# A graph layer on one core: seven parts instead of six, and every unit in eight steps

## The chip, the cores and the metric

The kernel runs on one core of a Trainium2 chip. The engines that matter are TensorE (PE; its weight loads are shown as PEld), VectorE (DVE), ScalarE (ACT), GpSimd (POOL) and SyncE (SP), whose queue issues nearly all the plain transfers; GpSimd issues the indirect ones. The metric is the device time of one execution in microseconds, the median of the runs shown. The profile is of one execution, with a span from the first to the last instruction that is a little shorter than that execution's own time.

## The reference

The layer has 12500 nodes with 128 features and 412500 edges with 64 features. Edges are sorted by their destination `dst`; the attention of an edge depends on both its ends and its own features, the softmax runs over all the edges at once, and the weighted values are summed by source node. Two normalisations follow.

```python
h = x @ Wn + bn
q, k, v = x @ Wq + bq, x @ Wk + bk, x @ Wv + bv
eh = edge_attr @ We + be
attn_in = concatenate([q[src], k[dst], eh], axis=-1)
hmid = leaky_relu(attn_in @ A1 + b1, 0.2)
scores = leaky_relu(hmid @ A2 + b2, 0.2)          # 8 heads
w = softmax(scores.mean(axis=-1), axis=0)         # over all edges
out = segment_sum(w[:, None] * v[dst], src)
y = h + out
ref = gamma * (y - mean(y)) / sqrt(var(y) + 1e-5) + beta
result = layernorm(x + ref)
```

## The kernel before

A1 is multiplied into Wq, Wk and We beforehand, so that an edge's hidden layer is a sum of three terms: one of its source node, one of its destination node, one of its own features. The host pads the edges to 403 groups of 1024 (8 tiles of 128), and the nodes to 98 blocks of 128: node i belongs to block i mod 98.

The work has two halves that run beside each other.

*Making records* (`make`, L749 to 962), group by group in the order of `dst`. Since `dst` is sorted, a group's destinations lie in a short window of rows. A one-hot matrix (L799) and TensorE products (L854, L860 in `rows`) give, for each edge, its destination's k-term plus its edge term, and its v row. ScalarE copies these from PSUM to a record of 260 numbers (L871; L872 adds the source's place within its block). In the meantime VectorE counts, for every block, how many edges came before (L785 to L836): this gives each edge the row of its block's region to which its record goes. GpSimd then scatters the records, 128 rows of 1040 bytes at a time, to a table in DRAM, `rtab` (L883, eight scatters for a group). The pool of records has 6 buffers of four tiles.

*Units* (`sums_of`, L980 to 1311). Once all groups of a part are in the table, a unit takes two blocks' regions of it: a load `rt` (L1016), the sources' row `sl` (L1038), which TensorE turns (L1046), VectorE writes as bytes `slT` (L1053) and SyncE puts to DRAM (`put`, L1060) and reads back to all 128 partitions as `rowB` (`spread`, L1065). From this come one-hots in chunks of four tiles (L1074), hidden layers (L1085, L1094), leaky relu (L1105, L1109), scores (L1122 to L1155), a running maximum (L1165 to L1189), weights (L1194), the weighting of source one-hots (L1203, L1217), and the weighted sums of v (L1246), which are added to the sums of the part before (L1227 loads them, L1262 adds, L1269 stores).

The groups are cut into 6 parts of 73, 73, 73, 73, 62 and 49 groups (`CUTS`, L34). A block's region in a part has as many tiles as its mean number of edges plus 4.4 standard deviations need: 7, 7, 7, 7, 6 and 5. So units have 14, 12 or 10 tiles, and there are 6 x 49 = 294 of them. Two tables are used in turn (`TABS`), with 7 tiles a block. Rows that no record may reach are filled with zeros beforehand (`fill`, L513, and `fill_piece`, L526), all of it during the first part: 54 transfers of two blocks with 2 tiles each and 44 with 3. The first part also makes the tables of node terms (`tables`, L1495) and the places of the later edges (`later`), spread over nine tenths of its groups.

There is no scheduler: the order on each engine is the order of the program. Units are planned in *steps* (L983 to L1006): a unit's operations get numbers of steps from `s0`, the step of its first hidden layer. `e` is 1 for units of four chunks and 0 for those of three; it sets how many steps lie between one engine's work and the next one's that needs it. A unit of four chunks follows the one before after 8 steps, one of three after 6. `turn` is how many steps ahead of `s0` the row is turned: 11, or 8 where `e` is 0. A load may not come before a buffer of `rt` is free (`BLKS`, 6). The loop from L1566 runs through a part's groups, in six pieces each, and spreads the steps of the units of the part before evenly between them; the first part has no units beside it, and after the sixth part its units follow alone (the tail). `closing` (L1314) then scales, adds, normalises twice and writes out, seven blocks at a time, in buffers of `rt`.

Of the kernel before, what the change touches and what calls it, by code (L numbers as in the profile page):

```python
# [10 lines left out]
FP = mybir.dt.float32  # L11
# [9 lines left out]
P = 128  # L21
# [5 lines left out]
NB = 7  # L27
GT = 8
CG = 4
BLKS = 6  # L30
XA = 3
SPAN = 42
NP = 6
CUTS = 0, 0.1811, 0.3623, 0.5434, 0.7246, 0.8784, 1  # L34
TABS = 2
WIDTH = 14
HOLD = 7
LATE = 3
R = 4
WR = 260  # L40
# [3 lines left out]
class Plan:  # L44
# [4 lines left out]
    def __init__(self, n, e, nb, groups):  # L49
        self.n, self.e, self.nb, self.groups = n, e, nb, groups  # L50
        cut = [round(groups * c) for c in CUTS]
        self.parts = list(zip(cut[:-1], cut[1:]))


        def means(g0, g1):
            return [
                (min(e, g1 * GT * P) - g0 * GT * P) * max(0, -(-(n - b) // nb)) / n
                for b in range(nb)
            ]

        self.tiles = [
            max(-(-int(np.ceil(m + 4.4 * m**0.5)) // P) for m in means(*part))
            for part in self.parts
        ]
        most = max(self.tiles)
        self.cap = most * P
        self.trash = GT * P
        self.rows = nb * self.cap + self.trash


        self.fill = [
            [min(most, -(-int(most * P - m + 4.5 * m**0.5) // P)) for m in means(*part)]
            for part in self.parts[:TABS]
        ]
# [378 lines left out]
def sorted_path(  # L453
# [8 lines left out]
    nc = tc.nc  # L462
    nb = plan.nb
# [38 lines left out]
        nc.vector.memset(headsum[32 * j : 32 * j + 32, j : j + 1], 1.0)  # L502


    fmax = max(max(f) for f in plan.fill)
    empty = None

    def empties(pool):
        nonlocal empty
        empty = pool.tile([P, fmax, WR], FP, name="empty")  # L510
        nc.vector.memset(empty, 0.0)

    def fill(k, n):  # L513

        cap = plan.cap
        b = 0
        while b < nb:
            m = 1
            while m < n and b + m < nb and plan.fill[k][b + m] == plan.fill[k][b]:
                m += 1  # L520
            f = plan.fill[k][b]
            if f:
                yield b, m, f
            b += m

    def fill_piece(k, b, m, f):  # L526
        cap = plan.cap
        piece = nc.sync.dma_start(
            out=rtab[k][b * cap : (b + m) * cap, :]
            .rearrange("(b c) w -> b c w", b=m)[:, cap - f * P : cap, :]  # L530
            .rearrange("b (p k) w -> p b (k w)", p=P),
            in_=empty[:, :f, :]
            .rearrange("p (o k) w -> p o (k w)", o=1)
            .to_broadcast([P, m, f * WR]),
        ).ins
        if k == 0:
# [443 lines left out]
    def sums_of(bp):  # L980


        plans, s0, first, free, done, starts = [], 19, None, [], [], {}  # L983
        for p, bs, t in units:
            nt = len(bs) * t
            nk = -(-nt // 4)
            L, e = 2 * nk, int(nk > 3)
            turn = 11 if e else 8
            if plans:
                s0 += 2 * plans[-1][1]  # L990


            load_at = free[-BLKS] + 1 if len(free) >= BLKS else 0
            lead = turn + 8 if p in starts or p == 0 else turn + 8 + LATE
            s0 = max(s0, load_at + lead - 1)
            if first is not None:
                s0 = max(s0, first - (L + 5 + 3 * e))
            if len(done) > 1:
                s0 = max(s0, done[-2] + 1 - (L + 4 + 2 * e))
            f = s0 + L + 5 + 3 * e  # L1000
            load_at = max(load_at, s0 - lead)
            free.append(f + 3 + e + L)
            done.append(f + 4 + e + L)
            first = f + L
            starts.setdefault(p, load_at)
            plans.append((nt, nk, s0, load_at, f, e, turn))  # L1006
        steps = {}

# [264 lines left out]
        for i, (nt, nk, s0, load_at, f, e, turn_at) in enumerate(plans):  # L1273
# [33 lines left out]
        closing(bp, do, tail, f + 3 + e, f + 5 + e + 2 * j + 4)  # L1307
        order = lambda at: [(fn, args) for _, fn, args in sorted(at, key=lambda x: x[0])]
        return [order(steps.get(s, [])) for s in range(max(steps) + 1)], [
            starts[p] for p in range(NP)  # L1310
        ]


    def closing(bp, do, s0, s1, s2):  # L1314
# [6 lines left out]
        def three(b, k):  # L1321
            return b[:, k * NB * D : (k + 1) * NB * D].rearrange("p (b d) -> p b d", d=D)
# [78 lines left out]
        def fetch(st):  # L1401
            bl = st["bl"]
            rt = bp.tile([P, TM, WR], FP, name="rt").rearrange("p t w -> p (t w)")
            for k, (name, of) in enumerate((("hs", htab), ("part", atab[NP - 1]), ("xs", xtab))):
                st[name] = three(rt, k)
                nc.sync.dma_start(out=st[name], in_=of[:, bl, :])
            st["n1"], st["o"] = three(rt, 3), st["part"]

        def spread(st, y, k):
            if k == 1:  # L1410
# [155 lines left out]
    with tc.manual_schedule():  # L1566
        done = 0
        for p in range(NP + 1):
# [118 lines left out]
```

## Time and profile before

| | us |
|---|---|
| median of three runs (lowest, highest) | 5124.87 (5107.2, 5132.39) |
| profiled execution, own time | 5108.98 |
| its span | 5107.2 |
| PE, DVE, ACT, POOL busy | 4197.8, 3989.1, 3275.2, 3347.9 |
| first scatter; last scatter | 64.7; 4480.3 |
| masks made at a part's end (L920), first and last | 837.4; 4478.4 |
| last load of a unit; end | 4927.0; 5107.2 |

An engine's busy time is a share of the whole span, and stages have different limits, so the busy time by stretch says more than the page's first line. A group's line gives its count, its busy time, the mean of one in ns, and after the second bar the time that the engine was idle just before it, with what ended most of that time; "issue" there means that the profile shows nothing that it waited for. Matmuls overlap, so TensorE's busy share is not its share of work. A row of a stretch gives its ends, its length, each engine's busy time with the number of instructions, the granted clock, the share of the DMA engines and their rate in GB/s.

### The profile page before, as it was taken

Reading aid. Unit: us, or ns where it says so; the run is one execution under the profiler, and the core shown is the slowest. Engines: PE = TensorE matmul, PEld = TensorE weight load, DVE = VectorE, ACT = ScalarE, POOL = GpSimd, SP = SyncE. Lnnn points to the kernel's source line nnn. Section 1 sums busy time; section 2 is a strip of 40 time slices with the busy share of each in tenths; the row PEclk is TensorE's granted clock in tenths of the full one; section 3 lists DMA queues with packets and bytes.
Section 4 is the critical chain, followed back from the end, with each engine's and each line's share of the span. In section 5 each row is a group of like instructions: output and inputs, shape, how many; then the busy total and the mean of one; then the engine's idle time right before and its main releaser. Section 6 shows DMA issues by size and latency. Waiting matters only on the chain.

```text
span 5107.2 us, 97900 instructions
## 1 busy us (share of the span) xinstructions
PE 4197.8 (82%) x32676; PEld 3121.7 (61%) x32676; DVE 3989.1 (78%) x10011; ACT 3275.2 (64%) x8487; POOL 3347.9 (66%) x3265
## 2 busy tenths in 40 slices
PE   4556564998998989998999998999999899988880
PEld 2333332666766767776766776677777676666660
DVE  7666663888887888888888887888888788766678
ACT  2333331666766777776777776777777677766776
POOL 3777777777777777777777777777767566611002
PEclk7666665999999999999999999999999999999995
DMA  5889895988888998998988998998998898878763
GB/s 188 281 277 314 292 336 175 323 297 296 298 302 278 316 316 308 316 304 297 322 310 306 314 314 286 315 318 311 318 316 301 291 307 305 293 248 265 247 232 139
DMA packets 589700, 1477.77 MB, mean 289 GB/s; under 512 B 102746, under 2 KB 315629, under 8 KB 587392
## 3 DMA queue, kind: packets, MB, share of 16 engines
q1 hardware_dynamic: 434224, 1042.03, 62.4%
q0 software_dynamic: 154752, 429.39, 22.0%
q8 instruction: 259, 4.24, 0.3%
q14 instruction: 257, 2.11, 0.1%
q10 hardware_dynamic: 208, 0.00, 0.0%
HBM read 890.36 MB, written 580.68 MB: 288 GB/s over the span
## 4 chain that ended last, share of the span: by engine, by line
DMA 35%; PE 19%; POOL 16%; DVE 14%; issue 9%; ACT 7%; SPq 1%; ACTq 0%; DVEq 0%; POOLq 0%
DMA rtab<-rec,idx 18%; POOL rtab L883 16%; DMA row<-slT 6%; DMA rt<-rtab 5%; PE psm L1246 4%; DMA rowB<-row 4%; PE ph L1094 3%; PE pkv L860 3%; ACT rec L871 2%; PE ph L1085 2%; ACT ohw L1217 2%; PE pkv L854 2%; DVE hm L1109 2%; PE psm L1155 2%; PE psc L1122 1%
## 5 line engine op out<-in xcount | busy, mean ns | idle before, releaser
L883 POOL DMA_INDIRECT rtab<-rec,idx x3224 | 3287.0, 1020 | 1190.9 <-issue 789.4
L871 ACT ACTIVATE rec<-pkv 128x1024 f32<-128x1024 f32 x806 | 821.6, 1019 | 1125.1 <-DMA rtab<-rec,idx 789.5
L1217 ACT ACTIVATE ohw<-ohs,w 128x128 f32<-128x128 bf16 x3822 | 1259.5, 400 | 13.2 <-PE psm L1246 1.4
L1246 PE MATMUL psm<-rt,ohw 128*128 128x128 f32 x7644 | 1150.3, 293 | 8.9 <-ACT ohw L1217 7.5
L1246 PEld LDWEIGHTS psm<-rt,ohw 128*128 128x128 f32 x7644 | 983.5, 198 | 104.2 <-ACT hm L1105 31.3
L1105 ACT ACTIVATE hm<-ph 128x512 f32<-128x512 f32 (+1 forms) x1078 | 583.4, 541 | 473.3 <-PE ph L1094 466.8
L854 PE MATMUL pkv<-kvs,ohd 128*128 128x256 bf16 x3224 | 550.0, 299 | 402.9 <-ACT rec L871 378.9
L1094 PE MATMUL ph<-ohT,qs 128*128 128x512 bf16 (+3 forms) x4116 | 819.6, 321 | 39.6 <-DVE ohT L1074 39.4
L1109 DVE TENSOR_TENSOR hm<-ph,hm 128x512 f32<-128x512 f32 (+1 forms) x1078 | 668.0, 620 | 114.9 <-ACT hm L1105 114.5
L860 PE MATMUL pkv<-WeS,eat 64*128 64x128 f32 x6448 | 658.7, 329 | 0.0
L854 PEld LDWEIGHTS <-ohd 128*128 128x128 bf16 x3224 | 321.8, 105 | 542.2 <-issue 453.1
L1085 PE MATMUL ph<-ident,rt 128*128 128x128 f32 x3822 | 622.5, 281 | 14.3 <-DVE hm L1109 13.5
L1074 DVE TENSOR_SCALAR ohT<-rowB,iotaP 128x512 bf16<-128x512 uint8 (+1 forms) x1078 | 521.8, 484 | 119.3 <-DMA rowB<-row 114.3
L860 PEld LDWEIGHTS pkv<-WeS,eat 64*128 64x128 f32 x6448 | 487.9, 213 | 201.1 <-issue 199.0
L1094 PEld LDWEIGHTS <-qs 128*128 128x128 bf16 x4116 | 395.3, 100 | 173.4 <-issue 50.8
L1085 PEld LDWEIGHTS ph<-ident,rt 128*128 128x128 f32 x3822 | 477.2, 152 | 22.5 <-DVE hm L1109 17.9
L823 DVE TENSOR_TENSOR ats<-pc,oh 128x792 f32<-128x792 f32 x403 | 392.3, 973 | 106.1 <-PE pc L805 103.5
L1203 DVE TENSOR_TENSOR ohs<-iotaE,sl 128x512 bf16<-128x512 bf16 (+1 forms) x1078 | 415.0, 385 | 51.2 <-ACT ohw L1217 50.3
L1155 PE MATMUL psm<-headsum,z 128*128 128x4 f32 (+1 forms) x2156 | 286.4, 254 | 146.0 <-DVE z L1145 65.7
L834 DVE TENSOR_REDUCE pos<-ats 128x8 f32<-128x792 f32 x403 | 389.9, 967 | 3.4
L1155 PEld LDWEIGHTS psm<-headsum,z 128*128 128x128 f32 (+1 forms) x2156 | 273.9, 198 | 176.9 <-DVE z L1145 79.1
L1122 PE MATMUL psc<-hm,A2s 128*32 128x512 f32 (+3 forms) x2352 | 319.5, 533 | 12.8 <-DVE slT L1053 7.0
(151 smaller groups left out, 4080.8 us busy)
## 6 DMA issues: line engine op xcount, KB each, us to landing
rt<-rtab SPq DMA_DIRECT2D x196, 1820.0 KB
eat<-in_ea SPq DMA_DIRECT2D x201, 512.0 KB
rt<-rtab SPq DMA_DIRECT2D x49, 1560.0 KB
rt<-rtab SPq DMA_DIRECT2D x49, 1300.0 KB
qs<-qtab SPq DMA_DIRECT2D x294, 192.0 KB
rtab<-rec,idx POOLq DMA_INDIRECT x3224
dstb<-dtab SPq DMA_DIRECT2D x201, 256.0 KB
rowB<-row SPq DMA_DIRECT2D x196, 224.0 KB
```

The source lines that it names most:

```text
L854: nc.tensor.matmul(pk[:, h, i, :], ohd[:, t * P : (t + 1) * P], kvs, start=(i == 0), stop=False,)
L860: nc.tensor.matmul(pk[:, h, i, :D], eat[h * DE : (h + 1) * DE, (j + i) * P : (j + i + 1) * P], WeS[h * DE : (h + 1) * DE, :], start=False, ...
L871: nc.scalar.activation(rec[:, :, :, : 2 * D], pk, AF.Copy)
L883: one_tile = nc.gpsimd.indirect_dma_start(out=rtab[p % TABS][:, :], out_offset=bass.IndirectOffsetOnAxis(ap=idxs[g][:, t : t + 1], axis=0) ...
L1074: nc.vector.tensor_scalar(st["oh"][k][:, : n * P], st["rowB"][:, t0 * P : (t0 + n) * P], iotaP, None, op0=ALU.is_equal,)
L1085: nc.tensor.matmul(ph[:, j * P : (j + 1) * P], st["rt"][:, t0 + j, :D], ident, is_transpose=True, start=(j == 0), stop=False,)
L1094: nc.tensor.matmul(ph[:, cols], st["qs"][:, j0 // t, s, :], oh[:, cols], start=False, stop=(s == 2 and j1 == t0 + n),)
L1105: nc.scalar.activation(hm, state[i]["ph", k][:, : n * P], AF.Copy, scale=SLOPE)
L1109: nc.vector.tensor_tensor(hm, ph[:, : n * P], hm, op=ALU.max)
L1155: nc.tensor.matmul(st["psS"][:, t0 + j : t0 + j + (nv - 1) * sw + 1 : sw], z[: 32 * nv, j * P : (j + 1) * P], headsum[: 32 * nv, :nv], sta ...
L1217: nc.scalar.activation(ohw[:, j, :], ohs[:, :, j], AF.Copy, scale=st["w"][:, t0 + j : t0 + j + 1])
L1246: nc.tensor.matmul(st["psS"][:, (1 + u) * P : (2 + u) * P], ohw[:, j, :], st["rt"][:, t0 + j, D : 2 * D], start=(k == 0), stop=(k == t - 1),)
```

## The change

The number of parts, their cuts, the margin and the number of buffers are new: 7 parts of 40, 51, 62, 62, 62, 63 and 63 groups, with a margin of 4.15 standard deviations and regions of 4, 5, 6, 6, 6, 6 and 6 tiles. Units have 8, 10 or 12 tiles, that is two or three chunks, and there are 7 x 49 = 343 of them; the sum of tiles over all units stays 3822. `rt` has 7 buffers of 12 tiles instead of 6 of 14. `e` is 1 for all units, a unit follows the one before after 8 steps whatever its size (with 4 more for each chunk that it has more), and `turn` is 14, 12 or 11 for two, three or four chunks.

Since the first two parts' regions are smaller than the largest, the filling is in two stages. During the first part the rows between the least that a block can receive and its part's own tiles are filled from a tile of zeros in SBUF, as before (98 transfers of two blocks, 2 tiles each). The tiles above that, which the table's next part uses, are filled later: during the second part for the first table (49 transfers of two blocks, 2 tiles each) and during the third part for the second one (49, 1 tile each), in the eighth to the five eighths of the part's pieces. Their source is a table of zeros in DRAM. The steps that must be done by a part's end are at least those up to the last load of the part before. In `closing`, `n1` and `o` use the tiles of `part` and `hs`, as `rt` is smaller now.

```diff
-BLKS = 6
+BLKS = 7
-NP = 6
-CUTS = 0, 0.1811, 0.3623, 0.5434, 0.7246, 0.8784, 1
+NP = 7
+CUTS = 0, 0.0993, 0.2258, 0.3797, 0.5335, 0.6873, 0.8437, 1
...
-            max(-(-int(np.ceil(m + 4.4 * m**0.5)) // P) for m in means(*part))
+            max(-(-int(np.ceil(m + 4.15 * m**0.5)) // P) for m in means(*part))
...
-    fmax = max(max(f) for f in plan.fill)
+    fmax = max(
+        max(plan.tiles[k] - plan.cap // P + max(plan.fill[k]), plan.cap // P - plan.tiles[k])
+        for k in range(TABS)
+    )
+    zeros = dram.tile([P, fmax, WR], FP, name="zeros")
...
         nc.vector.memset(empty, 0.0)
+        nc.sync.dma_start(out=zeros, in_=empty)
...
-            f = plan.fill[k][b]
-            if f:
-                yield b, m, f
+            a = plan.cap // P - plan.fill[k][b]
+            if a < top:
+                yield b, m, a, top - a
...
+    def fill_top(k, n):
+
+        top, most = plan.tiles[k], plan.cap // P
+        if top < most:
+            for b in range(0, nb, n):
+                yield b, min(n, nb - b), top, most - top
...
-            .rearrange("(b c) w -> b c w", b=m)[:, cap - f * P : cap, :]
+            .rearrange("(b c) w -> b c w", b=m)[:, a * P : (a + f) * P, :]
             .rearrange("b (p k) w -> p b (k w)", p=P),
-            in_=empty[:, :f, :]
+            in_=(empty if source is None else source)[:, :f, :]
...
-            L, e = 2 * nk, int(nk > 3)
-            turn = 11 if e else 8
+            L, e = 2 * nk, 1
+            turn = {2: 14, 3: 12, 4: 11}[nk]
             if plans:
-                s0 += 2 * plans[-1][1]
+                s0 += 8 + 4 * (nk - plans[-1][1])
...
+            ends[p] = load_at
...
-            starts[p] for p in range(NP)
+            max(starts[p] - HOLD, ends[p - 1] + 1) if p else 0 for p in range(NP)
...
-            st["n1"], st["o"] = three(rt, 3), st["part"]
+            st["n1"], st["o"] = st["part"], st["hs"]
...
-            until = 0 if p == 0 else starts[p] - HOLD if p < NP else len(steps)
+            until = 0 if p == 0 else starts[p] if p < NP else len(steps)
...
+            if 0 < p <= TABS:
+                pieces = list(fill_top(p - 1, 2))
+                fills = [
+                    (na // 8 + na * j // (2 * len(pieces)), (p - 1, *piece, zeros))
+                    for j, piece in enumerate(pieces)
+                ]
```

More of the change, by code (lines that the diff above doesn't have):

```diff
@@ L511, in empties @@
         nc.vector.memset(empty, 0.0)
+        nc.sync.dma_start(out=zeros, in_=empty)
     def fill(k, n):
-        cap = plan.cap
-        b = 0
+        b, top = 0, plan.tiles[k]
         while b < nb:
@@ L520, in fill, with fill_piece @@
                 m += 1
-            f = plan.fill[k][b]
-            if f:
-                yield b, m, f
+            a = plan.cap // P - plan.fill[k][b]
+            if a < top:
+                yield b, m, a, top - a
             b += m
-    def fill_piece(k, b, m, f):
+    def fill_top(k, n):
[3 more added lines that the diff above has]
+                yield b, min(n, nb - b), top, most - top
+    def fill_piece(k, b, m, a, f, source=None):
         cap = plan.cap
@@ L535, in fill_piece @@
         ).ins
-        if k == 0:
+        if k == 0 and source is None:
             tc.declare_no_dep(piece, group="rows0", reason="rows that no record has reached")
@@ L980, in sums_of @@
     def sums_of(bp):
-        plans, s0, first, free, done, starts = [], 19, None, [], [], {}
+        plans, s0, first, free, done, starts, ends = [], 19, None, [], [], {}, {}
         for p, bs, t in units:
```

## The prediction, made before the changed kernel ran

> **What bounds the kernel now.** I read the page first (engines by slice, costliest groups), then busy time by stretch, then what GpSimd waited for, then SyncE's queue and VectorE in order of time where GpSimd is not the limit.
>
> ```profile
> span 5107.2 us, 97900 instructions
> ...
> POOL 3777777777777777777777777777767566611002
> ...
> L883 POOL DMA_INDIRECT rtab<-rec,idx x3224 | 3287.0, 1020 | 1190.9 <-issue 789.4
> ```
>
> GpSimd sends 3224 scatters (8 for each of 403 groups). Its slices stand at 7 up to the 28th and fall only afterwards. 7 is full here, as the waits show (stretch 1610 to 3146, then 3866 to 4478):
>
> ```profile
> POOL rtab L883 <- issue: 287.2, 942, 0.3
> ...
> POOL rtab L883 <- issue: 88.9, 291, 0.5
> POOL rtab L883 <- ACT rec L872: 79.6, 47, 6.7
> ```
>
> In the first stretch nearly all its idle time is a 0.3 us gap ahead of each scatter; with 0.96 us of work that is 1.265 us, and 1.31 on average: 10.51 us for a group's eight. In the second stretch it waits for records too. Last scatters of the six parts start at 869, 1639, 2405, 3173, 3873 and 4480 us: 73 groups take 766 to 770, but 62 take 700 (10.51 x 62 would be 652) and 49 take 607 (515). So GpSimd's rate sets the first four parts, units of 14 and 12 tiles set the fifth and sixth, and 627 us follow with no scatter. The stretches:
>
> ```profile
> 66.00:440.00 374.00, 217.05 (x1174) 142.59 (x1175) 262.52 (x469) 141.53 (x178) 287.82 (x260) 0.68 0.84 281
> 440.00:760.00 320.00, 194.25 (x1010) 125.26 (x1010) 200.02 (x399) 99.74 (x157) 247.11 (x239) 0.66 0.94 322
> 760.00:837.00 77.00, 36.44 (x212) 24.06 (x211) 31.99 (x61) 19.63 (x34) 59.02 (x60) 0.51 0.49 165
> ...
> 2378.00:3146.00 768.00, 701.76 (x5773) 529.34 (x5773) 650.56 (x1598) 554.62 (x1470) 589.96 (x585) 0.96 0.90 309
> 3146.00:3866.00 720.00, 675.92 (x5496) 510.23 (x5495) 610.79 (x1528) 538.38 (x1442) 515.62 (x512) 0.96 0.90 310
> 3866.00:4478.00 612.00, 561.53 (x4578) 420.78 (x4577) 481.83 (x1233) 433.23 (x1180) 400.07 (x396) 0.97 0.88 300
> 4478.00:4927.00 449.00, 388.60 (x2952) 300.75 (x2949) 301.05 (x939) 316.64 (x947) 31.81 (x17) 0.96 0.76 250
> ```
>
> The last columns are clock, DMA share and GB/s. What paces the sixth part and the tail is a loop through two small transfers:
>
> ```profile
> 4107.65 0.34 SPq L1060 DMA_DIRECT2D row<-slT  x1
> ...
> 4113.98 0.32 SPq L1065 DMA_DIRECT2D rowB<-row  x1
> ...
> 4118.35 0.48 DVE L1074 TENSOR_SCALAR ohT<-rowB,iotaP 128x512 bf16<-128x512 uint8 x1 [0.88 <-DMA rowB<-row]
> 4118.75 0.27 DVE L1053 TENSOR_SCALAR slT<-psc 12x128 uint8<-12x128 f32 x1
> ...
> 4119.05 0.32 SPq L1060 DMA_DIRECT2D row<-slT  x1
> ```
>
> A unit's row goes out, must land before it is read back to 128 partitions, the first one-hot waits for that, and only then does VectorE make the next unit's row. Over the sixth part 6.4 + 5.3 + 0.7 = 12.4 us, its whole unit period (12.5); in the tail 4.0 + 4.0 + 0.7 = 8.7 of 9.0.
>
> **The change, part by part.** All sums go by the profiled execution, span 5107.2 us (its own time is 5109.0; the median of the runs shown, 5124.9, lies 0.3% above).
>
> *First part, 73 to 40 groups.* It has no units beside it. 33 fewer groups are 264 scatters. GpSimd alone: the part's 583 intervals take 804 us, 67 above 1.265 each. That surplus sits on the table-making (two scatters that meet a subtraction of the tables take over 2.1 us), which stays, so 320 x 1.265 + 60 = 465. Bytes: before, 73 x 1.52 (records, features, indices, rows) + 64 of fills + 49 of tables = 224 MB (the rows give 221). After: 61 + 52 (98 fills of 520 KB) + 49 = 162, all but 6 in 36 groups. At the 322 GB/s of the row 440:760, 484 us, and 42 for the last four groups: 526. At 350, about what the fullest 20 us stretches hold (344 to 376), 488. VectorE has 495 - 33 x 4.06 (a group's seven operations: 0.97, 0.97, 0.76, 0.55, 0.37, 0.27, 0.17) = 361 us of work: hidden. Take 500, from 465 to 550; its last scatter starts at 565 instead of 869.
>
> *Second part, 51 groups beside 49 units of 8 tiles.* Scatters 51 x 10.51 = 536. Bytes 78 + 49 x 1.52 = 152 MB. New: 49 copies of 520 KB from a table of zeros in DRAM, in half of this part. No row shows DRAM to DRAM. Counted once, that half moves 102 MB in 268 us, 382 GB/s: at 340, +33 us; at 375, +5; counted as read and write, 128 MB, +109. I take +40, nearest to the count that the page's bytes use: 576. Each copy also stands in SyncE's queue ahead of the next rows and loads: 0.5 us of issue (the fills' median), 49 of them 25 us in a queue that mostly waits; behind a copy still in flight, the row's read-back has waited for a transfer only 14 us in 1610:3146 (L1065 for rt). Nothing added for it; were that cover gone, rival 2's price.
>
> *Third part, 62 groups, units of 10.* 652; 26 MB/2 of copies bring its half to 332 GB/s: +8 (0 to +30): 660.
>
> *Parts four to seven: 62, 62, 63, 63 groups beside units of 12.* 652 and 662 by scatters, period 13.3 us a unit. Per group there are 9.4 tiles, as in the parts of 73, so engines and DMA (205 MB, 314 GB/s against 309) are as full as at 2378:3146. 98 fewer chunks of one-hots (980 for 1078) pay for 49 more units. The seventh buffer takes away the wait of a load for a free buffer (SyncE's L1016 waits 180 us for sums in 1610:3146). The loop of 12.4 fits under 13.3 with 0.9 to spare. +5 each (0 to +40): 657, 657, 667, 667. The margin of 4.15 moves only the caps; the rule that a part ends after the last load of the one before it moves nothing here (step 387 against 384).
>
> Last scatter: 565 + 576 + 660 + 2 x 657 + 2 x 667 = 4449, against 4480. The four wide parts recover what was lost beside the 62 and 49 groups; the copies and denser fills eat most of the shorter start.
>
> *Tail.* 49 units of 12 tiles instead of 10. TensorE is busy 388.6 of 449 us, 7.8 a unit: with 12 tiles 9.4. The loop gives some 8.9 (rowB grows from 160 to 192 KB). The two-step spacing should take away TensorE's waits for the scores (47 us here), but not the loop, since the next unit's row is made in the same step as the first one-hot, behind it, before and after. So 9.4 (9.05 to 10.86, all scaled), 48 x 0.35 = +17: 644 after the last scatter. The closing's shared buffers (n1 over part, o over hs) write over tiles whose last reader stands ahead of them in the order of steps: nothing.
>
> Sum: 4449 + 644 = 5093, 14 less than before. Own time 5095; raised by the 0.3% that the median before lies above its profile, 5110.
>
> **The rivals** (times on the median's footing).
> 1. *The gain is kept.* DMA never sets the pace: 465, 541, 652, 653, 653, 663, 663, tail 635: 65 + 4290 + 635 = 4990, as a median 5005. For it: 322 GB/s held for 320 us while groups took 10.6 us. Against: at GpSimd's pace the new first part needs 350 and half the second 382.
> 2. *The row loop sets parts four to seven.* It decides from 13.3 us a unit, 0.9 above the sixth part's. At 14.0, 49 x 14.0 = 686 a part: +29 twice, +19 twice, some 10 in the third, 106 in all: 5215, slower. For it: in the fifth part (310 GB/s) the loop was 6.3 + 6.0 + 1.4 = 13.7, and rt came late there and in the sixth (35 times, 55 us). Against: 0.7 of that was a step between one-hot and next row that units of 12 do not have, and row and rt are larger in units of 14.
> 3. *Transfers set the first parts.* First part 526, second +109, third +30: 117 more than forecast, 5225. It decides where these stages get under 320 GB/s. The Trainium skill, "DMA: Bandwidth & Descriptors" (Specifications), gives an HBM limit of about 358 GB/s per core, which a copy within DRAM would load on both sides; by it, as an estimate, that half of the second part takes 128 MB / 358 = 357 us, +89 where I take +40. The trace does not bear it out as a hard limit (376 GB/s in 380 to 400 us), and no run here has such a copy.
> 4. *The tail stays as loose as before*, 10.4 us a unit: +48, 5160.
>
> A block overflowing its smaller cap would start the second path; the inputs' fullest blocks (484 of 512, 599 of 640, 725 of 768) exclude it.
>
> **How the numbers follow.** Forecast (5070 to 5150) 0.40; kept 0.25; loop 0.17; transfers 0.12; tail 0.06. What a measurement can tell from no change is about 0.5%, 26 us: below 5099 the forecast has 0.16 of its 0.40, within 0.20, above 0.04. Faster 0.16 + 0.25 = 0.41; slower 0.04 + 0.17 + 0.12 + half of the tail's = 0.36; within 0.23. For eight in ten, 4990 (all but the end of rival 1) to 5225 (most of 2 and 3).
>
> **What would show it.** First part's last scatter near 565; second part 576, with DMA share near 1 in its first half; parts four to seven with GpSimd's gaps "issue" alone at 10.6 us a group; row to row 13.4 us there; a tail period of 9.4. Records waited for by GpSimd in parts four to seven would be rival 2; a last scatter later than 4480, or a unit period over 10 in the tail, makes the forecast wrong.

## The result, and the profile after

The changed kernel takes 5179.3 us (median of 4 runs, 5169.6 to 5186.4), the kernel before in the same session 5128.6. The ratio is 1.0117, with a 95% interval of 1.0099 to 1.0136: slower by 1.2%. The forecast was 5110, no change within what can be told. The time lies inside the range given for eight in ten (4990 to 5225), but outside the forecast's own 5070 to 5150, and both signs that were named for a wrong forecast are there: the last scatter starts after 4480, at 4509, and a unit of the tail takes 10.04 us.

From the page of the changed kernel, the span, GpSimd's busy tenths by slice and the DMA totals (before 1477.77 MB), and from its list of groups the scatters':

```profile
span 5184.7 us, 98509 instructions
...
POOL 2666766677777777777777777777777777611002
...
L894 POOL DMA_INDIRECT rtab<-rec,idx x3224 | 3298.0, 1023 | 1209.2 <-issue 757.4 <-ACT rec L883 146.1 <-DMA rtab<-empty 61.5
...
DMA packets 658349, 1528.11 MB, mean 295 GB/s; under 512 B 108541, under 2 KB 359056, under 8 KB 656035
```

A scatter is what it was (1023 ns for 1020). GpSimd's slices at 6 and below are now at the left end (a slice is 130 us), where the two short parts are. By starts of last scatters, each part's length against the forecast:

| part (groups) | forecast | after | us a group | loads wait, us a unit |
|---|---|---|---|---|
| 1 (40) | 500 | 523.5 | 13.09 | - |
| 2 (51), units of 8 | 576 | 600.4 | 11.77 | 3.09 |
| 3 (62), units of 10 | 660 | 664.2 | 10.71 | 1.62 |
| 4, 5 (62), units of 12 | 657, 657 | 653.9, 665.2 | 10.55, 10.73 | 1.23, 1.31 |
| 6, 7 (63), units of 12 | 667, 667 | 672.3, 665.0 | 10.67, 10.56 | 1.09, 1.19 |
| tail, units of 12 | 644 | 675.4 | - | 0.70 |

The last column is VectorE's mean idle time ahead of `sl` (L1050), the first operation that reads a loaded block, taken from the operations' gaps in the trace, without the first two and the last two units of a row. The last scatter starts at 4509, forecast 4449. The 92 us between the forecast's sum of 5093 and the span of 5184.7 are 23 in part 1, 24 in part 2, 4 + 8 in parts 3 to 7, 31 in the tail, and 2 of rounding off.

Busy time by stretch: two of the first part, two of the second, one of a wide part, and 400 us of the tail (columns as before: clock, DMA share, GB/s last).

```profile
66.00:220.00 154.00, 84.56 (x410) 54.19 (x410) 111.38 (x194) 61.76 (x65) 95.24 (x84) 0.69 0.92 311
220.00:360.00 140.00, 82.92 (x394) 54.79 (x396) 103.44 (x189) 53.18 (x63) 87.73 (x80) 0.70 0.96 310
...
700.00:980.00 280.00, 216.24 (x1602) 152.07 (x1600) 177.75 (x455) 145.83 (x392) 179.44 (x180) 0.87 0.93 316
980.00:1176.00 196.00, 165.55 (x1254) 115.62 (x1253) 144.60 (x371) 113.89 (x311) 143.09 (x143) 0.91 0.82 278
...
3161.00:3817.00 656.00, 609.02 (x4962) 447.36 (x4961) 540.49 (x1332) 455.01 (x1232) 504.59 (x492) 0.98 0.91 314
...
4560.00:4960.00 400.00, 370.66 (x2577) 273.75 (x2578) 262.40 (x717) 263.77 (x792) 27.93 (x13) 0.97 0.75 256
```

In the second part no engine is full: TensorE 216 of 280, VectorE 178, GpSimd 179, and the DMA engines move 316 GB/s, less than the 322 that they held before. That points to a chain of waits, and the waits of that stretch name it (total, times, longest):

```profile
DVE sl L1050 <- DMA rt<-rtab: 73.6, 18, 9.9
...
POOL rtab L894 <- ACT rec L883: 35.2, 8, 7.4
```

VectorE stands still for loads, and the work for GpSimd's next record stands behind it in VectorE's order. One load in order of time:

```profile
779.80 0.37 SPq L1028 DMA_DIRECT2D rt<-rtab  x1
784.54 0.32 SPq L1072 DMA_DIRECT2D row<-slT  x1
790.28 0.17 DVE L1050 SCALAR_TENSOR_TENSOR sl<-mask,rt 128x8 bf16<-128x8 bf16 x1 [3.55 <-DMA rt<-rtab]
...
792.79 0.43 SPq L1028 DMA_DIRECT2D rt<-rtab  x1
```

The load is issued at 779.8, is there 10.5 us later, and VectorE has by then stood at `sl` for 3.55 us. The order of steps issues a load five steps ahead of its `sl`. A unit has eight steps, so in the second part, which goes through 49 units, a step has 600/392 = 1.53 us, and five of them 7.7 us. Before, with 73 groups beside 49 units, it was 770/392 = 1.96 us, five 9.8. The change made the step shorter and left the distance in steps as it was.

### The profile page after: what moved, and what is told of

Read it like the earlier page. It is cut to its first block, busy times and chain, and to the rows that moved or that the text cites. A ratio compares the mean times of both kernels' runs of the same rounds, so it can differ in the third digit from the quotient of the medians.

```text
span 5184.7 us, 98509 instructions
## 1 busy us (share of the span) xinstructions
PE 4295.4 (83%) x32727; PEld 3126.5 (60%) x32727; DVE 3940.6 (76%) x9968; ACT 3192.4 (62%) x8438; POOL 3359.7 (65%) x3265
## 2 busy tenths in 40 slices
DMA packets 658349, 1528.11 MB, mean 295 GB/s; under 512 B 108541, under 2 KB 359056, under 8 KB 656035
## 3 DMA queue, kind: packets, MB, share of 16 engines
HBM read 945.65 MB, written 614.80 MB: 301 GB/s over the span
## 4 chain that ended last, share of the span: by engine, by line
DMA 43%; DVE 19%; PE 18%; POOL 5%; issue 5%; ACT 4%; SPq 2%; DVEq 0%; ACTq 0%; POOLq 0%
DMA rt<-rtab 23%; DMA rtab<-rec,idx 8%; DMA row<-slT 8%; POOL rtab L894 5%; PE psm L1258 5%; DMA rowB<-row 3%; PE psc L1134 2%; PE ph L1106 2%; DVE hm L1121 2%; PE ph L1097 2%; DVE ohT L1086 2%; DVE pos L845 2%; PE pkv L871 2%; DVE ohd L810 1%; DVE ohs L1215 1%
## 5 line engine op out<-in xcount | busy, mean ns | idle before, releaser
L894 POOL DMA_INDIRECT rtab<-rec,idx x3224 | 3298.0, 1023 | 1209.2 <-issue 757.4
L1258 PEld LDWEIGHTS psm<-rt,ohw 128*128 128x128 f32 x7644 | 1001.3, 201 | 95.3 <-ACT ohw L1229 57.0
L1117 ACT ACTIVATE hm<-ph 128x512 f32<-128x512 f32 (+1 forms) x980 | 564.4, 576 | 600.8 <-PE ph L1106 599.0
L1106 PE MATMUL ph<-ohT,qs 128*128 128x256 bf16 (+2 forms) x3822 | 817.3, 337 | 8.8 <-DVE ohT L1086 7.7
L871 PE MATMUL pkv<-WeS,eat 64*128 64x128 f32 x6448 | 621.4, 315 | 0.0
L865 PE MATMUL pkv<-kvs,ohd 128*128 128x256 bf16 x3224 | 525.2, 289 | 68.3 <-ACT rec L882 63.6
L1086 DVE TENSOR_SCALAR ohT<-rowB,iotaP 128x512 bf16<-128x512 uint8 (+1 forms) x980 | 484.8, 495 | 115.1 <-DMA rowB<-row 113.1
L871 PEld LDWEIGHTS pkv<-WeS,eat 64*128 64x128 f32 x6448 | 458.9, 201 | 187.9 <-issue 180.4
L1134 PE MATMUL psc<-hm,A2s 128*32 128x384 f32 (+2 forms) x2744 | 401.9, 488 | 127.2 <-DVE slT L1065 125.1
L1050 DVE SCALAR_TENSOR_TENSOR sl<-mask,rt 128x12 bf16<-128x12 bf16 (+2 forms) x343 | 61.0, 178 | 526.1 <-DMA rt<-rtab 525.4
L1106 PEld LDWEIGHTS <-qs 128*128 128x128 bf16 x3822 | 376.2, 100 | 124.3 <-issue 22.4
```

The lines of the kernel that those rows point to most:

```text
L865: nc.tensor.matmul(pk[:, h, i, :], ohd[:, t * P : (t + 1) * P], kvs, start=(i == 0), stop=False,)
L871: nc.tensor.matmul(pk[:, h, i, :D], eat[h * DE : (h + 1) * DE, (j + i) * P : (j + i + 1) * P], WeS[h * DE : (h + 1) * DE, :], start=False, ...
L894: one_tile = nc.gpsimd.indirect_dma_start(out=rtab[p % TABS][:, :], out_offset=bass.IndirectOffsetOnAxis(ap=idxs[g][:, t : t + 1], axis=0) ...
L1086: nc.vector.tensor_scalar(st["oh"][k][:, : n * P], st["rowB"][:, t0 * P : (t0 + n) * P], iotaP, None, op0=ALU.is_equal,)
L1106: nc.tensor.matmul(ph[:, cols], st["qs"][:, j0 // t, s, :], oh[:, cols], start=False, stop=(s == 2 and j1 == t0 + n),)
L1117: nc.scalar.activation(hm, state[i]["ph", k][:, : n * P], AF.Copy, scale=SLOPE)
```

## The experiments

Two theories stood against each other for each stage: *lateness* (loads and rows issued too few steps ahead) and *size* (bytes in the first two parts, TensorE's 12 tiles in the tail). The first three runs and the last seven fell on chips whose profile shows a mean granted clock of 0.83 to 0.85 (0.89 to 0.92 in the others), where the kernel before takes 6045 to 6160 us and GpSimd waits for records in every part; of these only the tail, where their clock is 0.96 to 1.00 as elsewhere, is held against other chips' runs.

**The tail: turn, load, spacing.** The three edits, one kernel each; the first puts the next unit's row two steps earlier, the second issues the loads six steps earlier, the third goes back to one step between engines and six steps a unit in the last part alone.

```diff
-            turn = {2: 14, 3: 12, 4: 11}[nk]
+            turn = {2: 14, 3: 14, 4: 11}[nk]
```


> The changed kernel with units of 12 (and 10) tiles turned 14 steps ahead instead of 12, so that the next unit's row is made two steps before the first one-hot and no longer behind it; row, read-back and load move ahead with it. Lateness theory (the loop row out, read back, one-hot, next row paces the tail at 10.0 us a unit): the tail's period falls to about 9.3 us, 30 to 35 us less over 48 units, and parts three to seven lose 2 to 5 us each, since their loop of 13.4 us touches the scatters' 13.3; the whole 40 to 55 us less than the changed kernel. Rival, size theory (TensorE's work for 12 tiles paces the tail, 92% busy): tail period 9.9 to 10.1, the whole within 10 us of the changed kernel.

```diff
-            lead = turn + 8 if p in starts or p == 0 else turn + 8 + LATE
+            lead = turn + 14 if p in starts or p == 0 else turn + 14 + LATE
```


> The changed kernel with each unit's load six steps earlier, nothing else moved; seven buffers allow it. Lateness theory (VectorE waits for rt, 3.1 us a unit in the second part and 1.1 to 1.6 in parts three to seven, because five steps are now shorter than a load): those waits go; the second part falls from 600 to about 560 us, parts three to seven from 664, 654, 665, 672, 665 by 3 to 10 us each, the tail by 5 to 15: some 60 to 80 us less. Rival, bytes theory (transfers at 93% share pace the second part): the second part stays above 590 us, as an earlier load only queues longer, and the whole is within 15 us of the changed kernel.

```diff
-            L, e = 2 * nk, 1
-            turn = {2: 14, 3: 12, 4: 11}[nk]
+            L, e = 2 * nk, int(p < NP - 1)
+            turn = {2: 14, 3: 12, 4: 11}[nk] if e else 8
...
-                s0 += 8 + 4 * (nk - plans[-1][1])
+                s0 += 8 + 4 * (nk - plans[-1][1]) if e or plans[-1][5] else 2 * nk
```


> The changed kernel with the last part's units planned as before the change: one step between engines, six steps a unit, turned 8 steps ahead. Size theory (12 tiles' work and the row loop, which is the same in both plans, pace the tail): tail period 9.8 to 10.5, the whole within 15 us of the changed kernel. Rival, the two-step spacing itself costs (longer drain of 48 steps, psum and buffers held longer): period 9.3 or less, 30 us or more off. If the two steps do help as meant, the period rises to 10.6 or more.

Unit periods in the tail, from row to row (L1072) without the first two units and the last one: 9.83, 9.84 and 10.25 us, against 10.04 of the changed kernel (ratios to before on that chip 1.020, 1.018 and 1.0185). VectorE's waits for transfers in 400 us of the tail, of the changed kernel (4560 to 4960), and of the first and the second experiment (5650 to 6050):

```profile
DVE sl L1050 <- DMA rt<-rtab: 27.2, 21, 3.7
DVE ohT L1086 <- DMA rowB<-row: 24.6, 23, 2.6
```

```profile
DVE sl L1050 <- DMA rt<-rtab: 62.3, 35, 4.3
```

```profile
DVE ohT L1086 <- DMA rowB<-row: 35.2, 33, 2.7
```

Each edit ends one of the two waits, and the other grows. With both periods at 9.83 I read this as TensorE's size, and that was a mistake, as a later run shows: each edit only uncovered the other's lateness. The third one shows that the looser steps are not what makes the period longer than the 9.4 of the forecast, as the old plan is 0.2 us a unit slower. It does not price the two steps by themselves, since the old plan also moves the row and the load; in the same 400 us VectorE waits 95.3 us for the row and 53.3 for loads there.

**Loads early, on a chip of the usual clock.** The changed kernel again as control, the loads six steps earlier, no copies (all filling from SBUF in the first part), and the 54 subtractions of the table-making left out (each bf16 part is then the rounded value itself).

> The changed kernel itself again, beside the kernel before, as the measure for the three others of this group: 1.010 to 1.014 of the kernel before, with last scatters of its parts near 588, 1189, 1853, 2507, 3172, 3844 and 4509 us if TensorE's clock is granted as in the first profile. Nothing is tested by it alone.

> The loads six steps earlier, beside the changed kernel this time. Lateness theory: VectorE's waits for rt go, the second part falls from 600 to 560 to 575 us, parts three to seven by 3 to 10 us each, the tail by 5 to 10 us; 50 to 80 us less than the changed kernel. Bytes theory: the second part stays above 590 us and the whole within 15 us of the changed kernel.

```diff
-    zeros = dram.tile([P, fmax, WR], FP, name="zeros")
+    zeros = None
...
-        b, top = 0, plan.tiles[k]
+        b, top = 0, plan.cap // P
...
-            if 0 < p <= TABS:
+            if False:
```


> The changed kernel with all of each block's unreached rows filled in the first part from SBUF, as before the change, and no copies from a table of zeros later: 39 MB of writes move from parts two and three to the first. Bytes theory for the first part (524 us at 310 GB/s): it grows by 39 MB / 320 GB/s = 120 us, to 630 to 650. Rival, chain theory (the table-making's ping-pong between ScalarE and VectorE, squeezed into 36 groups, paces it): it grows by less than 60 us. In the second part, without copies: 550 to 560 by the bytes theory, 585 or more by the lateness theory.

```diff
-                less = np_.tile([P, NB, 2, D], FP, name=f"less{s}")
-                less = less[:, :, :half, :]
-                nc.vector.tensor_tensor(less, rest, to[s], op=ALU.subtract)
-                rest = less
```


> The changed kernel whose table-making leaves out the 54 subtractions between the three bf16 parts of a row (each part is then the rounded value itself), with every copy and transfer kept. Chain theory: without ScalarE and VectorE waiting for one another, and without the stretched scatters beside the subtractions, the first part falls from 524 to 480 us or less. Bytes theory: its 162 MB still go at 310 to 320 GB/s, and it stays at 505 or more. Nothing else changes, so the whole falls by what the first part falls.

| | ratio (95%) | part 1 | 2 | 3 | 4 to 7 | tail |
|---|---|---|---|---|---|---|
| control | 1.0117 (1.0089 to 1.0146) | 521 | 592 | 659 | 2653 | 675 |
| loads early | 0.9969 (0.9955 to 0.9984) | 521 | 537 | 653 | 2640 | 673 |
| no copies | 1.0144 (1.0124 to 1.0163) | 590 | 541 | 655 | 2653 | 671 |
| no subtractions | 1.0062 (1.0042 to 1.0081) | 500 | 589 | 659 | 2649 | 672 |

One line takes 75 us off. The second part goes at GpSimd's own pace (10.54 us a group) with all its copies in place: 537 us, under the 560 to 575 that the lateness theory gave. Its stretch 600 to 860, that of the control first, then that of the early loads:

```profile
600.00:860.00 260.00, 201.11 (x1457) 137.55 (x1454) 165.14 (x417) 131.41 (x344) 177.89 (x177) 0.87 0.92 315
```

```profile
600.00:860.00 260.00, 218.90 (x1648) 151.05 (x1648) 187.38 (x471) 146.53 (x388) 199.66 (x199) 0.88 1.01 360
```

315 GB/s was what the late loads let through, and no limit: 360 are moved once they come early. Bytes are refuted as the bound of the second part. Yet without the copies its length is 541 with the old distance too, where the lateness theory had asked for 585 or more. So copies and a short distance cost some 50 us only together. The traces show how. From the first copy of the second part to its last, the control and the early loads have:

```profile
650.00:957.00 307.00, 235.07 (x1734) 164.46 (x1733) 195.81 (x500) 157.45 (x421) 198.59 (x198) 0.87 0.93 322
```

```profile
632.00:910.00 278.00, 235.68 (x1817) 165.38 (x1816) 203.77 (x518) 162.08 (x439) 213.65 (x212) 0.91 1.02 366
```

While copies run, a group takes 12.4 us in the control and 10.5 with early loads; in the rest of the part 10.9 and 10.55. Where VectorE stood waiting for more than 0.5 us, a load's length can be read as the time from its issue to its `sl`: in the control a median of 10.2 us while copies run and 9.0 in the rest of the part, and 9.1 in the run without copies. The copies lengthen loads that have nothing to spare, and this part of the delay comes after the issue, not from SyncE's queue. Without them VectorE's wait for loads falls from 3.1 to 2.05 us a unit (gaps ahead of `sl`). GpSimd's wait for records follows: from 640 to 1100 it is 42.9 us in the control and 1.2 with early loads.

In the first part both theories missed. All the filling there costs that part 69 us for 39 MB (120 by the bytes theory, under 60 by the other), which says that transfers count; leaving out the subtractions takes 21 off it, to 500 (480 or less by the chain theory, 505 or more by the other), which says that the tables' chain counts too. A version with the copies left out and nothing in their place gave no time, since it reads rows that nothing has written.

**Row and load early together, tables spread, and two parts of the change alone.** First: both one-line edits shown. Second: the same, with the tables and fills of the first part spread over all of its pieces instead of nine tenths. Third: the kernel before with two steps between engines for all units. Fourth: the changed kernel with six buffers.

> The changed kernel with loads six steps earlier (as in lead6b) and, for units of 12 tiles, the next unit's row 14 steps after the load of the sums instead of 12. In lead6b no group of VectorE waits for loads any more, and what is left in the wide parts is the one-hot's wait for the row read back (208 us from 1840 to 4480). Theory A (the row loop is what costs the wide parts and the tail now): that wait falls under 60 us, the parts of 62 and 63 groups from 653-667 to 645-660 us, the tail's unit period from 9.84 to 9.4-9.6 us; 5050 to 5075 us, ratio 0.990 to 0.994. Theory B (GpSimd's scatters set the wide parts, TensorE's 12 tiles the tail): VectorE's wait goes and nothing follows from it, parts within 5 us of lead6b's, period 9.8, 5080 to 5100 us.

```diff
-            n0 = na * 9 // 10
+            n0 = na
```


> lead6_turn14 with the work on the tables of the first part spread over all of its 40 groups instead of the first nine tenths. Theory 'bytes and subtractions bunched': the first part (521 us) gets 5 to 20 us shorter, the other parts stay, 5 to 20 us off lead6_turn14. Theory 'chain of the record building': the first part within 5 us of 521 and the time the same; if the tables' last entries come too late for the second part, that part starts later by as much.

```diff
-            L, e = 2 * nk, int(nk > 3)
-            turn = 11 if e else 8
+            L, e = 2 * nk, 1
+            turn = {3: 12, 4: 11}[nk]
...
-                s0 += 2 * plans[-1][1]
+                s0 += 8 + 4 * (nk - plans[-1][1])
```


> The kernel before with one piece of the change alone: two steps between engines and eight steps of spacing for all units, those of 12 and 10 tiles of the sixth part and the tail too (row 12 steps after the load); the six parts, six buffers and 14 tiles stay. Theory (the loop through the row paced the sixth part, 12.4 us, and part of the tail): sixth part 607 to 585-600, tail's unit period 9.05 to 8.7-8.9, 15 to 35 us off, ratio 0.993 to 0.998. Rival (the looser steps buy nothing, since the row is still made behind the one-hot, and the closing starts two steps later): ratio 1.000 to 1.006.

```diff
-BLKS = 7
+BLKS = 6
```


> The changed kernel with six record buffers instead of seven. Theory (the lateness of the loads is a fixed number of steps ahead of their use, and a buffer lives about 44 of the 48 steps that six buffers allow, so the seventh buys nothing by itself): within 0.3% of the changed kernel, ratio 1.009 to 1.015, second part 590 to 605 us. Rival (the seventh buffer is what lets loads start early enough): second part 620 to 660, third to seventh 10 us longer each, ratio over 1.02.

| | ratio (95%) | part 1 | 2 | 3 | 4 to 7 | tail | period there |
|---|---|---|---|---|---|---|---|
| row and load early | 0.9876 (0.9859 to 0.9892) | 523 | 545 | 648 | 2627 | 648 | 9.31 |
| and tables spread | 0.983 (0.9813 to 0.9846) | 500 | 543 | 650 | 2631 | 647 | 9.25 |
| six buffers | 1.0113 (1.0091 to 1.0135) | 521 | 597 | 664 | 2659 | 666 | 9.91 |

With both early, 5058.5 us against 5122.5: more than the lateness theory had asked for. In the tail VectorE waits for neither transfer any more, and TensorE is full (400 us of the tail with row and load early, then with the tables spread too; columns as in the rows above):

```profile
4470.00:4870.00 400.00, 388.96 (x2797) 292.97 (x2796) 274.17 (x774) 285.65 (x861) 25.27 (x12) 1.00 0.78 273
```

```profile
4450.00:4850.00 400.00, 389.84 (x2814) 293.13 (x2813) 278.53 (x778) 287.34 (x865) 25.14 (x12) 1.00 0.78 273
```

97% against 371 of 400 in the changed kernel, and a period of 9.3, close to the 9.4 that the forecast had as TensorE's size. The four wide parts lose 13 us by early loads and 13 more by the early row. In 1840 to 4360 VectorE's wait for loads was 238.6 us in the changed kernel; with loads early it waits 187.2 for the row instead; with both 48.5:

```profile
DVE sl L1050 <- DMA rt<-rtab: 238.6, 115, 12.4
```

```profile
DVE ohT L1086 <- DMA rowB<-row: 187.2, 88, 17.5
```

```profile
DVE ohT L1086 <- DMA rowB<-row: 48.5, 12, 15.9
```

Spreading the tables takes 23 us off the first part, a little more than the bunching theory gave (5 to 20). The last version, three lines off the changed kernel, is at 5037.0 us 1.7% faster than the kernel before.

Six buffers cost the changed kernel nothing: the wait for loads in 1840 to 4360 stays at

```profile
DVE sl L1050 <- DMA rt<-rtab: 239.3, 119, 8.5
```

Two steps alone, in the kernel before, gave 1.0048 (1.0031 to 1.0065), where 0.993 to 0.998 was expected: the theory missed, and the rival's 1.000 to 1.006 came. The sixth part went from 607 to 637 us, the tail's period from 8.95 to 9.19. The waits of 3880 to 4478, before and then in this run:

```profile
POOL rtab L883 <- ACT rec L872: 75.2, 45, 6.7
DVE sl L1038 <- DMA rt<-rtab: 54.9, 35, 3.4
DVE ohT L1074 <- DMA rowB<-row: 43.4, 30, 4.9
```

```profile
DVE sl L1038 <- DMA rt<-rtab: 110.5, 37, 5.7
POOL rtab L883 <- ACT rec L872: 96.7, 48, 6.3
...
DVE ohT L1074 <- DMA rowB<-row: 7.9, 15, 1.0
```

The row's wait went, as two steps promise, and the loads' wait doubled: eight steps a unit instead of six make each step shorter, and the load is still five of them ahead (by the plan of the kernel before, its six buffers hold nearly all loads of 12 and 10 tiles to five).

**The same with earlier loads, and the seventh buffer under them.** The run of two steps alone with the loads of its units of 12 and 10 tiles three steps earlier, which six buffers allow; and row and load early with six buffers.

```diff
-            lead = turn + 8 if p in starts or p == 0 else turn + 8 + LATE
+            early = 11 if nk == 3 else 8
+            lead = turn + early if p in starts or p == 0 else turn + early + LATE
```


> before_e1 (the kernel before with two steps between engines for units of 12 and 10 tiles) with the loads of these units three steps earlier, which six buffers just allow (48 steps of life). In before_e1 VectorE waited 2.4 us a unit for loads in the sixth part, which took 637 us, 30 more than before. Theory (late loads are what made two steps cost): that wait falls under 0.8 us, the sixth part to 585-610 us, the tail's period from 9.19 to 8.6-8.9; ratio 0.992 to 0.999. Rival (the length of the chain of steps itself): wait gone or not, sixth part within 10 us of 637, ratio 1.002 to 1.007.

> lead6_turn14 with six record buffers instead of seven. A buffer then has to live some 53 steps where six buffers of units eight steps apart give 48, so the planner spaces the units of 12 tiles nearly nine steps apart. Theory A (the seventh buffer is what earlier loads need): the wide parts go back to 655-672 us and the tail's period to 9.8 or more; ratio 1.000 to 1.010. Theory B (a step is only as long as its work, so nine lighter steps take the time of eight): within 0.4% of lead6_turn14, ratio 0.985 to 0.991.

Both ran three times, always on a chip of the low clock, so that the ratios expected of them could not be tested; the third time beside the fastest version as control.

> The same kernel as before_e1_lead3. Its tail was read already (period 8.90 us, VectorE's wait for loads 0.07 us a unit). Theory (late loads are what made two steps cost): sixth part 585-610 us against 637 in before_e1, ratio 0.992 to 0.999. Rival (the longer chain of steps itself): sixth part within 10 us of 637, ratio 1.001 to 1.006.

> The same kernel as lead6_turn14_b6. Its tail's period was 10.09 us, against 9.31 with seven buffers, some 38 us over 48 units. Theory A (seven buffers are needed by earlier loads everywhere): parts of 62 and 63 groups 655-672 us besides, ratio 1.000 to 1.010. Theory B (in the parts with scatters nine lighter steps take the time of eight, only the tail needs seven): parts within 5 us of lead6_turn14's 648-663, ratio 0.994 to 0.998.

> lead6_turn14_all again, as control for the next run. On a chip like that of its first run: ratio 0.982 to 0.985, wide parts 650 to 664 us, tail's period 9.25. On a chip of the lower clock (0.84), where records are late in all parts and VectorE does not wait for loads: theory (earlier loads take away only waits for loads) ratio 1.005 to 1.015, tail's period 9.3, wide parts as in turn14 and lead6 there (about 850); rival (earlier loads help there too, by denser steps) ratio under 1.000.

> lead6_turn14_b6 for the third time. Theory A (seven buffers are needed by earlier loads everywhere): parts of 62 and 63 groups 8 us or more over the control's on the same chip, tail's period 10.0 against 9.3; 60 to 110 us over the control (20 of them the control's denser first part). Theory B (only the tail needs seven): parts within 6 us of the control's, 50 to 65 us over it.

> before_e1_lead3 for the third time. On a chip like before_e1's: theory (late loads made two steps cost) sixth part 585 to 610 us against 637, total 20 to 45 us under before_e1's ratio of 1.005; rival (the longer chain itself) within 10 us of 637. On a chip of the lower clock only the tail's period (8.9) can be read.

Ratios in that order: 1.0084, 1.0309, 1.0033, 1.0269, 1.008, 1.032 and 1.0052. Read from the tails: two steps with earlier loads have a period of 8.90, 8.97 and 8.88 us against 9.19, with VectorE's wait for loads at 0.05 to 0.09 us a unit against 0.92, as the lateness theory said, and end where the kernel before was (8.95): in units of 10 tiles two steps buy nothing. Whether late loads were all of the 30 us in the sixth part stays open, as there the records set the pace on these chips (716 to 752 us). With six buffers under row and load early, the tail's period is 10.33 against 9.33 of the fastest version on the same chip, and the five parts of 62 and 63 groups take 82 us more (4358 to 4275); in all 147 us, where 60 to 110 was expected. So the seventh buffer is needed under the earlier loads, and idle without them. What makes those five parts longer is not shown, since VectorE does not wait for loads in either.

On that chip the control is 0.8% slower than before (1.006 to 1.010; 1.005 to 1.015 was expected for such a chip), not 1.7% faster. Its last scatter starts at 5563.6 us; in the 6-part kernel beside it, with two steps, at 5566.6: records come at some 13.7 us a group in both, so shorter first parts save nothing, and the 7 parts' longer tail (660 to 625 us) remains.

## Why the prediction was wrong, point by point

*First part: "Take 500, from 465 to 550".* 523, inside its bounds and 23 too low. The 500 lay between a sum for 322 GB/s and one for 350; the rows show 311 and 310. It was sized for transfers and GpSimd as if the tables' work had room, and that work is packed into nine tenths of 40 groups. With it spread over all of them the part takes 500, with the subtractions left out 500 too, and with 39 MB more of fills 590: transfers and the tables' chain both count.

*Second part: "I take +40, nearest to the count that the page's bytes use: 576".* This is the step that failed first. 600, and not by bytes. A rate was forecast where a distance in steps decided: with early loads the part takes 537 with the copies in it, so their price as traffic is the lower end of the range ("at 375, +5") or less. The high count of read and write, and rival 3's price with it, fall too. That the copies cost 51 us in the changed kernel (592 to 541), not far from the +40, is luck: the price came from a rate of 340 GB/s, and 366 were moved once loads came early.

*"The loop of 12.4 fits under 13.3 with 0.9 to spare", parts four to seven.* Right in the main as a time: 2656 us for 2648, period 13.4, GpSimd's gaps mostly "issue". Rival 2 did not happen: from 1853 to 4509 GpSimd waited 17.1 us for records in all. The +5 each that I added is about what the two short distances cost there: with early loads the four parts take 2640, with the row early too 2627. The reading of the loop was weak, though. Its three pieces run from one row to the next, so they add up to the unit period whatever sets it: in the third part of the kernel before, which the scatters set, they are 5.6 + 7.9 + 1.9 = 15.4 us, the whole period as well. And the new rule for a part's end moves nothing only for the second part (step 387 against 384); by the plan each later part ends three steps later (782 against 779, and so on), and what that costs was not measured.

*"The seventh buffer takes away the wait of a load for a free buffer".* False as a gain. In the changed kernel loads go out at a fixed distance ahead of their use, not when a buffer comes free; six buffers give the same time.

*Tail: "The loop gives some 8.9", so TensorE's 9.4.* Period 10.0, +31 us. TensorE's 9.4 was right as a size (9.25 to 9.31 once nothing else is late). What failed was the loop's 8.9. A step of 1.25 us puts a load 6.3 us ahead of its `sl`; from issue to `sl` it was 7.5 us in the old tail and is 8.5 now (medians). The loop was priced without the load, though in the old tail (4500 to 4927) VectorE already waited as long for loads as for rows:

```profile
DVE ohT L1074 <- DMA rowB<-row: 39.0, 31, 3.4
DVE sl L1038 <- DMA rt<-rtab: 38.2, 37, 2.5
```

Rival 4 (10.4) was nearest in its number; its reason, steps as loose as before, gave 10.25 in the run that made them so.

What I had seen and passed over stands in the text of rival 2: `rt` came late in the fifth part and in the sixth, 35 times there. It was the row of before that showed the fault; in the fifth part (3180 to 3860):

```profile
DVE sl L1038 <- DMA rt<-rtab: 59.2, 35, 8.0
```

In that part a step had 700/392 = 1.79 us, five 8.9, and VectorE lost 1.1 us a unit ahead of `sl` (0.25 to 0.33 in the parts of 73 groups, at five steps of 9.8). By the forecast's own 576 us the change was to bring the second part's step to 1.47 us, and this got no price.

The direction hangs on the loads: with them early the ratio is 0.997. With the row early and the tables spread as well, the same 7 parts run at a span of 5036, 57 below the sum of 5093.

## What to carry to other kernels

Where prefetch distance is written in steps of a software pipeline, turn it into microseconds whenever a change alters how much work a step holds, and hold it against the transfer's time from the trace; a change that makes steps shorter shortens every prefetch with it. Two lags in one loop hide each other: when removing one moves the wait to the other at the same period, remove both before calling the engine the limit. A spare buffer is worth nothing until something is issued early enough to use it.

## What the runs showed of the hardware

The DMA engines moved 360 GB/s over 260 us, with copies from DRAM to DRAM among loads and scatters, and single 20 us stretches reached 387:

```profile
720.00:740.00 20.00, 17.88 (x124) 12.75 (x124) 14.42 (x36) 11.89 (x33) 15.43 (x16) 0.83 1.04 385
740.00:760.00 20.00, 18.77 (x160) 13.63 (x160) 17.79 (x46) 13.48 (x36) 15.73 (x15) 1.00 1.04 387
```

The prediction weighed the 358 GB/s of the Trainium skill's "DMA: Bandwidth & Descriptors" (Specifications) as a limit. The same page (Bandwidth) says that this is the share with both cores of a memory domain streaming, and that one core alone reached 425. The runs agree with that second sentence, and not with 358 as a limit here. These rates count a copy once: the run without copies moves the same bytes (1527.82 MB for 1528.11) and reads 39.1 MB less from DRAM (906.51 for 945.65). Counted on both sides, the 278 us of the second part's copies with early loads moved 102 + 26 MB, some 460 GB/s.

A scatter on GpSimd gets longer while VectorE subtracts one SBUF tile from another (128x1792, fp32 result). The scatters' group from 66 to 360 us, in the changed kernel and without the subtractions:

```profile
L894 POOL DMA_INDIRECT rtab<-rec,idx x163 | 185.0, 1135 | 172.6 <-ACT rec L883 63.0 <-DMA rtab<-empty 61.5 <-issue 36.9
```

```profile
L894 POOL DMA_INDIRECT rtab<-rec,idx x175 | 172.3, 984 | 119.5 <-ACT rec L883 53.3 <-issue 44.7 <-DVE ns L1531 17.1
```

1135 ns against 984. The Trainium skill's "GPSIMD Engine Reference" (Key points) says that GpSimd shares its SBUF interfaces with VectorE and contends with instructions of two SBUF inputs; the runs agree, at 0.15 us a scatter on average.

And the chips of the low clock: one wide part's stretch of the fastest version there, where TensorE's granted clock is 0.85 (0.99 in its first run) and the tail's 1.00:

```profile
3000.00:3800.00 800.00, 661.68 (x4517) 482.28 (x4567) 499.61 (x1224) 422.93 (x1139) 458.29 (x461) 0.85 0.69 238
5640.00:6040.00 400.00, 385.74 (x2742) 291.51 (x2785) 276.62 (x772) 284.70 (x858) 23.51 (x11) 1.00 0.77 267
```

Which of two orders of work was the faster one went with that clock (0.983 on one chip, 1.008 on the other). That the clock is the cause is not shown, and why it is granted so was not followed.
